# Two layers of MoE, attention and a gated recurrence: the recurrence as a pipeline over its blocks, its final state's product made once, loads and fills in another order, experts in a fixed order

## The chip, the cores and the metric

The kernel runs on one NeuronCore of a Trainium2 chip. Its engines are TensorE (PE, matrix products into PSUM), VectorE (DVE), ScalarE (ACT), GpSimd (POOL) and SyncE (SP, which here only issues DMAs); POOL issues DMAs too. The metric is the device time of one execution in microseconds, lower is better. All data are float32, and the profile shows each matmul of this kernel, other than the 128-column transposes, as two records.

## The reference, cut to what matters

x holds 2 x 2048 tokens of 256 values. Six sublayers are added to it in turn; the first and third, and the fourth and sixth, are the same function with the same weights.

```python
x = x + 0.5 * L0_ffn(layernorm(x))     # MoE: 6 experts, the best 2 per token, and a shared expert
x = x +       L0_attn(layernorm(x))    # attention, 16 heads, 2048 keys
x = x + 0.5 * L0_ffn(layernorm(x))
x = x + 0.5 * L1_ffn(layernorm(x))     # gated recurrence
x = x +       L1_attn(layernorm(x))    # causal attention with rotary and relative positions
x = x + 0.5 * L1_ffn(layernorm(x))
```

The recurrence runs over the first axis of x, which has only two entries, so it has two steps; each of the 2048 columns is on its own:

```python
def step(c, xt):
    ft = sigmoid(xt @ wf.T + c @ uf.T + bf)
    it = sigmoid(xt @ wi.T + c @ ui.T + bi)
    gt = tanh(xt @ wc.T + c @ uc.T + bc)
    return ft * c + it * gt
h = tanh(x @ wo.T + c_final @ uo.T + bo)   # c_final is the same for both steps
```

The MoE picks two experts per token, weights their outputs `(silu(x @ w1.T) * (x @ w3.T)) @ w2.T`, and adds a shared expert of the same form for every token.

## The kernel before

x stays in SBUF for the whole program, as 32 chunks of 128 tokens by 256 values; four chunks are a block (512 tokens), and there are eight blocks, four per batch entry. The stages follow one another in the order of the reference.

**Order of the work.** The program is traced in Python and a planner puts each engine's instructions in order: it simulates the program with estimated costs and at each point takes, of what is ready, what was written first. Inside `manual_schedule` the engines named there keep the written order. In the MoE that is PE alone, so DVE, ACT, POOL and SP are planned; the two attentions fix PE, ACT and DVE; the recurrence fixes none. SP and POOL are planned everywhere, and each engine executes its list in order. SBUF is taken in pools that are stacked: a pool that is opened where another was closed waits for the readers of the old one.

**MoE** (`first_moe`, `moe`; run twice). Tokens are treated in two halves of 16 chunks. `stats` and `norm` make the layer norm of a block and its transpose; `route` picks the experts; `sort` gives each (token, choice) a place in a list ordered by expert and scatters the normalised rows there with 32 indirect DMAs from POOL (L276) into `places`, a DRAM buffer. That buffer is set to zero once, by two DMAs from POOL at the start of the program (L1099), since some places stay empty. `shared` (up: L102, L290, L291) and `shared_down` (L299, L304) are the shared expert of a block. `experts` runs over 37 tiles of 128 places: load (L322, SP), transpose (L325, L327), up (L332, L337, L339), transpose of h (L344, L346), down (L351, L357), store to `results` (L358). `combine` gathers each token's two results with 32 indirect DMAs per half (L376, POOL) and adds them to x (L383, DVE). The written order is: halves' norms and routing with shared blocks 0 to 4 between, experts and combine of half 0, experts of half 1, shared blocks 5 to 7, combine of half 1.

**Recurrence** (`recurrence`; run twice). First six products give the gates' bias from the initial state (L694, L698). Then block after block (`cb`, the tokens of both steps): `layernorm_T` for both steps (L78 to L94), six gate banks a step (L102 from L719's loop, ACT at L719), the state on DVE (L722 to L731), and for each of 8 output chunks a sum in one bank of wo by x (L739), uo by the final state (L744) and a one-row product for the bias (L748); then tanh (L750) and the addition to x (L753). PSUM is used as three double banks and two single ones.

**Before attention 1.** Its weights are loaded, and two DRAM buffers `skew` are filled by 32 DMAs from POOL (L1144) ahead of the first recurrence. The recurrence's 13 weights are loaded in a pool of their own at the start of each of the two runs (L69).

Of the kernel before, what the change touches and what calls it, by code (L numbers as in the profile page):

```python
# [10 lines left out]
F32 = mybir.dt.float32  # L11
# [6 lines left out]
P = 128  # L18
# [24 lines left out]
def macaron_kernel(ctx: ExitStack, tc: tile.TileContext, t: dict, out: bass.AP):  # L43
# [5 lines left out]
    ones_row = const.tile([1, P], F32, name="ones_row")  # L49
    nc.vector.memset(ones_row, 1.0)  # L50
# [5 lines left out]
    nc.sync.dma_start(out=krow, in_=t["krow"])  # L56
# [6 lines left out]
    for b in range(NTB):  # L63
        nc.sync.dma_start(out=x[:, ts(b, CPB), :], in_=x_in[:, ts(b, CPB), :])

# [5 lines left out]

    def layernorm_T(c0, dst, lnp, psp, copy):


        mv = lnp.tile([P, CPB, 2], F32, name="mv")
        for c in range(CPB):
            st = lnp.tile([P, nc.vector.BN_STATS_DIM], F32, name="bnst")
            nc.vector.bn_stats(out=st, in_=x[:, c0 + c, :])  # L78
            nc.vector.bn_aggr(out=mv[:, c, :], in_=st)
        ve = lnp.tile([P, CPB], F32, name="ve")  # L80
        nc.gpsimd.tensor_scalar_add(ve, mv[:, :, 1], EPS)
        rstd = lnp.tile([P, CPB], F32, name="rstd")
        nc.gpsimd.tensor_tensor(rstd, ve, mhalf, ALU.pow)
        pair = psp.tile([P, 2, TB], F32, name="big")
        pts = [pair[:, kc, :] for kc in range(2)]
        for c in range(CPB):
            xn = lnp.tile([P, D], F32, name="xn")
            nc.vector.tensor_scalar(
                xn, x[:, c0 + c, :], mv[:, c, 0:1], rstd[:, c : c + 1], ALU.subtract, ALU.mult
            )  # L90
            for kc in range(2):
                nc.tensor.transpose(pts[kc][:, ts(c, P)], xn[:, ts(kc, P)], ident)
        for kc in range(2):
            copy(dst[:, kc, :], pts[kc])  # L94
# [16 lines left out]

    HB = NTB // 2
# [8 lines left out]
    def moe(w, ws, gate_w, gate_b, rev, tri, iota):  # L121
        with ExitStack() as s:
# [15 lines left out]
            mvs, rstds, oneh = {}, {}, {}  # L138
# [144 lines left out]
            def shared(b):  # L283
                pgu = [bank() for _ in range(4)]
                for i in range(4):
                    mm2(pgu[i], ws[:, :, i // 2 * D : i // 2 * D + D], ts(i % 2, P), xnT[b])
                hh = wk.tile([P, 2, TB], F32, name="hh", bufs=2)
                for ic in range(2):
                    sg = wk.tile([P, TB], F32, name="sgs", bufs=2)
                    nc.scalar.activation(sg, pgu[ic], AF.Silu)  # L290
                    nc.vector.tensor_tensor(hh[:, ic, :], sg, pgu[2 + ic], ALU.mult)  # L291
                return hh

            def shared_down(b, hh):
                for half in range(CPB // 2):
                    po = bank()
                    for c in range(2):
                        for ic in range(2):
                            nc.tensor.matmul(  # L299
                                po[:, ts(c, D)], lhsT=hh[:, ic, ts(half * 2 + c, P)],  # L300
                                rhs=ws[:, ic, 2 * D :], start=ic == 0, stop=ic == 1,
                            )
                    xs = x[:, ds(b * CPB + half * 2, 2), :].rearrange("p c d -> p (c d)")
                    nc.vector.scalar_tensor_tensor(xs, po, 0.5, xs, ALU.mult, ALU.add)  # L304

            def experts(h, exi):
# [54 lines left out]
                for i in range(NST + 2):  # L361
                    if i + 1 < NST:
                        tile_in(i + 1)
# [7 lines left out]
            def combine(h):  # L371
                for c in range(HC):
                    for i in range(2):
                        yg = wk.tile([P, D], F32, name="yg", bufs=6)
                        k = i * HC + c
                        nc.gpsimd.indirect_dma_start(  # L376
                            out=yg, out_offset=None, in_=results[h],
                            in_offset=bass.IndirectOffsetOnAxis(
                                ap=place[h][:, k : k + 1], axis=0
                            ),  # L380
                        )
                        xs = x[:, h * HC + c, :]
                        nc.vector.scalar_tensor_tensor(  # L383
                            xs, yg, weight[h][i][:, c, :], xs, ALU.mult, ALU.add
                        )

            with tc.manual_schedule(engines={mybir.EngineType.PE}):
                for b in range(HB):
                    stats(b)
                    norm(b)  # L390
                route(0)
                for b in range(HB, NTB):
                    stats(b)
                hh = [shared(0)]
                e0 = sort(0)
                for b in range(1, HB):
                    norm(HB + b - 1)
                    hh.append(shared(b))
                    shared_down(b - 1, hh[b - 1])
                norm(NTB - 1)  # L400
                route(1)
                hh.append(shared(HB))
                shared_down(HB - 1, hh[HB - 1])
                e1 = sort(1)
                shared_down(HB, hh[HB])
                experts(0, e0)
                combine(0)
                experts(1, e1)
                late = None
                for b in range(HB + 1, NTB):  # L410
                    hh = shared(b)
                    if late is not None:
                        shared_down(*late)
                    late = (b, hh)
                shared_down(*late)
                combine(1)
# [138 lines left out]
    ENGINES = {mybir.EngineType.PE, mybir.EngineType.Activation, mybir.EngineType.DVE}  # L555

# [123 lines left out]
    def recurrence(w):  # L680
        with ExitStack() as s:
# [3 lines left out]
            big = s.enter_context(tc.tile_pool(name="rec_big", bufs=3, space=PSUM))  # L685
            psp = s.enter_context(tc.tile_pool(name="rec_ps", bufs=2, space=PSUM))

            bias0 = {}
            for n in "fic":
                bias0[n] = keep.tile([P, 2], F32, name=f"bias0{n}")  # L690
                for m in range(2):
                    pb = psp.tile([P, TB], F32, name="ps1")
                    for kc in range(2):
                        nc.tensor.matmul(  # L694
                            pb[:, 0:1], lhsT=w[f"u{n}"][:, kc, ts(m, P)],
                            rhs=w["in_c"][:, kc : kc + 1], start=kc == 0, stop=kc == 1,
                        )
                    nc.vector.tensor_tensor(  # L698
                        bias0[n][:, m : m + 1], pb[:, 0:1], w[f"b{n}"][:, m : m + 1], ALU.add
                    )  # L700
            for cb in range(SB):
                xnT = []
                for step in range(2):
                    xt = wk.tile([P, 2, TB], F32, name=f"xnT{step}")
                    layernorm_T((step * SB + cb) * CPB, xt, lnp, big, nc.vector.tensor_copy)
                    xnT.append(xt)
                c1 = wk.tile([P, 2, TB], F32, name="c1")
                c2 = wk.tile([P, 2, TB], F32, name="c2")
                for step in range(2):
                    gate = {}  # L710
                    for n, fn in (("f", AF.Sigmoid), ("i", AF.Sigmoid), ("c", AF.Tanh)):
                        pg = big.tile([P, 2, TB], F32, name="big")
                        gate[n] = wk.tile([P, 2, TB], F32, name=f"g{n}")
                        for m in range(2):
                            mm2(pg[:, m, :], w[f"w{n}"], ts(m, P), xnT[step], stop=step == 0)
                            if step == 1:
                                mm2(pg[:, m, :], w[f"u{n}"], ts(m, P), c1, start=False)
                            bias = bias0[n] if step == 0 else w[f"b{n}"]
                            nc.scalar.activation(  # L719
                                gate[n][:, m, :], pg[:, m, :], fn, bias=bias[:, m : m + 1]  # L720
                            )
                    nc.vector.tensor_tensor(gate["i"], gate["i"], gate["c"], ALU.mult)  # L722
                    if step == 0:
                        for m in range(2):
                            nc.vector.scalar_tensor_tensor(
                                c1[:, m, :], gate["f"][:, m, :], w["in_c"][:, m : m + 1],
                                gate["i"][:, m, :], ALU.mult, ALU.add,
                            )
                    else:
                        nc.vector.tensor_tensor(c2, gate["f"], c1, ALU.mult)  # L730
# [507 lines left out]
```

## Time and profile before

| what | us |
|---|---|
| three runs | 4820.29, 4836.28, 4840.08 |
| median | 4836.28 |
| the profiled execution | 4831.55 |
| its span, first to last instruction | 4829.4 |

The stages in the profiled execution, cut where PE starts or ends them: start 0 to 42.5, first MoE to 413, way into attention 0 to 456.8, attention 0 to 2420, second MoE to about 2790, first recurrence from 2821.2 to 3066.6, attention 1 to 4563.3, second recurrence to 4829.4.

The profile's page gives each engine's busy time, the span in 40 slices with a digit of busy tenths, the granted TensorE clock, DMA queues, the chain of work that ended last, and groups of instructions with their mean duration and what they waited for. "L744 PE ... x4" is four instructions of line 744; a bracket at the end gives the idle time before them and the instruction that ended it. PEld is the load of weights into PE, which overlaps matmuls.

### The profile page before, as it was taken

The numbers are of one execution on the slowest core, as the hardware profiler recorded it, in microseconds if no ns is written. First come the engines' busy times: TensorE is split into PE (matmuls) and PEld (weight loads), VectorE is DVE, ScalarE is ACT, GpSimd is POOL, SyncE is SP. The second block draws the span as 40 slices with busy tenths as digits, with TensorE's granted clock in tenths as the row PEclk, the third lists the DMA queues.
The fourth block names the chain that finished last, engine by engine and source line by source line (L and its number), as shares of the span: only waits on it lengthen the run. The fifth ranks groups of instructions, "written<-read, shape, count | busy, mean of one in ns | idle before, by whom it ended". The sixth has DMA issues, their size and how long they took to land.

```text
span 4829.4 us, 74856 instructions
## 1 busy us (share of the span) xinstructions
PE 4579.8 (95%) x28768; PEld 2414.1 (50%) x28768; DVE 2649.7 (55%) x6138; ACT 2166.7 (45%) x4319; POOL 888.6 (18%) x925
## 2 busy tenths in 40 slices
PE   6996999999999999999989979899999999999999
PEld 3553544444444444444355535555555555555454
DVE  5234676767656667676452342356665555666421
ACT  2321465666655556566622211243544534445511
POOL 4315000002000000000043130343313344322000
PEclk9997999999999999999999989899999999999999
DMA  6331000000000000000033220244222244322100
GB/s 223 124 95 37 1 1 1 1 1 1 1 1 1 1 1 1 1 1 1 1 125 117 85 95 0 61 102 105 60 51 58 57 100 103 66 53 53 32 18 18
DMA packets 344904, 223.98 MB, mean 46 GB/s; under 512 B 146339, under 2 KB 324517, under 8 KB 344549
## 3 DMA queue, kind: packets, MB, share of 16 engines
q1 hardware_dynamic: 328324, 171.21, 14.0%
q0 software_dynamic: 16224, 47.99, 3.0%
q8 instruction: 229, 3.75, 0.3%
q14 instruction: 127, 1.03, 0.1%
HBM read 114.03 MB, written 105.12 MB: 45 GB/s over the span
## 4 chain that ended last, share of the span: by engine, by line
PE 88%; DVE 4%; POOL 3%; DMA 2%; issue 2%; ACT 0%; SPq 0%; POOLq 0%; DVEq 0%; ACTq 0%
PE s L615 15%; PE s L603 10%; PE acc L628 10%; PE s L852 7%; PE s L102 6%; PE s L937 6%; PE big L102 5%; PE acc L967 5%; PE s L332 5%; PE s L351 2%; PE ps L739 1%; PE ps L744 1%; DMA yg<-results,at 1%; PE s L547 1%; PE s L947 1%
## 5 line engine op out<-in xcount | busy, mean ns | idle before, releaser
L607 DVE TENSOR_REDUCE mx<-s 128x1 f32<-128x512 f32 x2048 | 1252.3, 683 | 597.7 <-PE s L603 597.5
L620 ACT ACTIVATE pT<-s 128x512 f32<-128x512 f32 x2048 | 1082.1, 601 | 628.5 <-PE s L603 582.9
L603 PE MATMUL s<-kT,q 32*128 32x512 f32 x4096 | 1249.9, 633 | 1.5 <-ACT q L596 1.4
L615 PE MATMUL s<-q,kT 32*128 32x512 f32 x4096 | 1231.7, 612 | 4.1 <-DVE q L512 4.1
L958 ACT ACTIVATE pT<-s 128x512 f32<-128x512 f32 (+3 forms) x1280 | 598.0, 544 | 500.0 <-PE s L937 290.6
L603 PEld LDWEIGHTS s<-kT,q 32*128 32x128 f32 x4096 | 539.2, 183 | 316.7 <-ACT pT L620 165.3
L852 PE MATMUL s<-kT,q 32*128 32x512 f32 (+6 forms) x3520 | 680.3, 473 | 9.7 <-POOL kT L790 7.4
L615 PEld LDWEIGHTS s<-q,kT 32*128 32x128 f32 x4096 | 500.5, 183 | 295.1 <-DVE mx L607 120.3
L860 DVE TENSOR_REDUCE mx<-s 128x1 f32<-128x512 f32 (+1 forms) x768 | 466.2, 677 | 253.7 <-PE s L852 234.3
L937 PE MATMUL s<-q,kT 32*128 32x512 f32 (+3 forms) x2048 | 522.3, 535 | 1.7 <-DVE s L991 1.7
L628 PE MATMUL acc<-pT,v 128*32 128x512 f32 x4096 | 492.3, 598 | 0.0
L852 PEld LDWEIGHTS s<-kT,q 32*128 32x128 f32 x3520 | 372.6, 188 | 110.4 <-ACT pT L958 31.7
L332 PE MATMUL s<-we,xT 128*128 x592 | 287.6, 609 | 0.9 <-ACT xT L327 0.9
L937 PEld LDWEIGHTS s<-q,kT 32*128 32x128 f32 x2048 | 231.6, 186 | 95.4 <-DVE mx L860 33.2
L967 PE MATMUL acc<-pT,v 128*32 128x512 f32 (+3 forms) x2560 | 268.5, 537 | 0.0
L628 PEld LDWEIGHTS acc<-pT,v 128*32 128x32 f32 x4096 | 107.2, 109 | 295.3 <-issue 294.1
L346 DVE COPY hT<-s 128x256 f32<-128x256 f32 x148 | 62.6, 424 | 292.7 <-PE s L344 292.7
L890 POOL TENSOR_TENSOR band<-band,mneg 128x640 f32<-128x640 f32 x128 | 160.9, 1260 | 313.9 <-DVE mneg L886 313.7
L876 DVE CUSTOM_DVE_ANT_0 band<-s,band 128x160 f32<-128x160 f32 (+1 forms) x512 | 155.5, 316 | 99.6 <-PE s L937 51.6
L147 POOL TENSOR_SCALAR ve<-mv 128x4 f32<-128x4 f32 x16 | 3.6, 226 | 1114.3 <-DVE mv L145 1110.3
L376 POOL DMA_INDIRECT yg<-results,at x128 | 121.5, 950 | 377.8 <-DMA results<-y 339.8
L351 PE MATMUL s<-we,hT 128*128 x592 | 157.1, 390 | 12.8 <-DVE hT L346 12.7
(209 smaller groups left out, 5052.5 us busy)
## 6 DMA issues: line engine op xcount, KB each, us to landing
band<-skew SPq DMA_DIRECT2D x32, 1280.0 KB, 6.6
pd<-band SPq DMA_DIRECT2D x32, 1280.0 KB, 8.1
xs<-places SPq DMA_DIRECT2D x148, 128.0 KB, 2.0
results<-y SPq DMA_DIRECT2D x148, 128.0 KB, 2.0
places<-zero POOLq DMA_DIRECT2D x2, 4736.0 KB, 36.2
we<-in_we SPq DMA_DIRECT2D x12, 768.0 KB, 10.2
skew<-s SPq DMA_DIRECT2D x32, 256.0 KB, 3.6
s<-pd SPq DMA_DIRECT2D x32, 256.0 KB, 3.5
```

Of the source, the lines that this page charges most:

```text
L102: nc.tensor.matmul(ps, lhsT=w[:, kc, cols], rhs=rhs[:, kc, :], start=start and kc == 0, stop=stop and kc == 1,)
L332: nc.tensor.matmul(pu, lhsT=xT[i][:, ts(kc, P)], rhs=w[:, kc, ds(val[i], 2 * D)], start=kc == 0, stop=kc == 1,)
L603: nc.tensor.matmul(ps, lhsT=q[t][rows(j), ts(qb, P)], rhs=kT[b, g][rows(j), ts(kc, TB)], start=True, stop=True,)
L607: nc.vector.tensor_reduce(mx[t][:, qb * J + j, kc : kc + 1], ps, AX.X, ALU.max)
L615: nc.tensor.matmul(st, lhsT=kT[b, g][rows(j), ts(kb, P)], rhs=q[t][rows(j), :], start=True, stop=True,)
L620: nc.scalar.activation(z.pTs[t, kb, j], st, AF.Exp)
L628: nc.tensor.matmul(z.acc[t][rows(j), :], lhsT=v[b, g // 2][:, kb, ds(h * VW, 32)], rhs=z.pTs.pop((t, kb, j)), start=kb == 0, stop=kb == NK ...
L852: nc.tensor.matmul(ps[:, ds(cols, n)], lhsT=lhsT, rhs=kT[b, c, g][rows(j), ds(k0, n)], start=True, stop=True,)
L860: nc.vector.tensor_reduce(m[:, c : c + 1], ps[:, 0:n], AX.X, ALU.max)
L937: nc.tensor.matmul(ps[:, q0:], lhsT=k, rhs=q[t][rows(j), q0:], start=True, stop=True, skip_group_check=True,)
L958: nc.scalar.activation(z.pTs[t, kb, j][:, q0:], st.pop((t, kb, j))[:, q0:], AF.Exp)
L967: nc.tensor.matmul(z.acc[t][rows(j), q0:], lhsT=v[b, kb // CPB, g // 2][:, kb % CPB, ds(h * VW, 32)], rhs=z.pTs.pop((t, kb, j))[:, q0:], s ...
```

## The change

- **Recurrence.** PE, ACT and DVE now run in written order. The layer norm (`normal`), its transposes (`turn`), the gates of one step and half of the state (`gate`), and the outputs are separate functions, written interleaved over blocks: gates of step 0 for the next block, layer norm of the one after, gates of step 1 for this block, outputs of the last block. The product of the final state with uo is made once a block in `final`, where DVE adds the bias (now stored for all 128 partitions), and DVE adds that sum to each step's product with wo; the one-row product is gone. All eight PSUM banks form one pool. In the second recurrence each pair of chunks is stored right after its last addition; before, the stores were written per block.
- **MoE.** PE, ACT and DVE in written order. The shared expert is cut into up, multiply and down; blocks 0 to 4 are put among the norms and routing. The combine of half 0 is written inside the experts of half 1, one chunk every second tile (`first_half`, from the fourth on); that of half 1 is spread among shared blocks 5 to 7.
- **Loads and fills.** The zero fill of `places` moves from POOL, ahead of everything, to SP, written behind the MoE's loads. Attention 0's weights are written behind the first MoE. The fill of `skew` moves from before the first recurrence, on POOL, to before the second MoE, on SP; the recurrence's first load of weights too is written before the second MoE. Attention 1's weights are allotted at the other end of SBUF.

```diff
-            with tc.manual_schedule(engines={mybir.EngineType.PE}):
+            with tc.manual_schedule(engines=ENGINES):
                 for b in range(HB):
                     stats(b)
                     norm(b)
+                    if b == 1:
+                        up(0)
                 route(0)
+                up(1)
+                mul(0)
+                e0 = sort(0)
+                mul(1)
+                down(0)
                 for b in range(HB, NTB):
+                    if b < NTB - 2:
+                        up(b - 2)
                     stats(b)
+                    norm(b)
+                    if b < NTB - 2:
+                        mul(b - 2)
+                        down(b - 3)
...
+                down(3)
+                up(4)
                 e1 = sort(1)
+                mul(4)
+                down(4)
+                experts(0, e0, lambda i: None)
+                experts(1, e1, first_half)
+                up(5)
+                mul(5)
+                up(6)
+                for c in range(6):
+                    combine(1, c)
+                down(5)
+                mul(6)
+                up(7)
+                for c in range(6, 11):
+                    combine(1, c)
+                down(6)
+                mul(7)
+                down(7)
+                for c in range(11, HC):
+                    combine(1, c)
...
+            def gate(cb, step, m):
+                g = {}
+                for n, fn in GATES:
+                    pg = bank()
+                    mm2(pg, w[f"w{n}"], ts(m, P), xnT[cb, step], stop=step == 0)
+                    if step == 1:
+                        mm2(pg, w[f"u{n}"], ts(m, P), c1[cb], start=False)
...
+            def final(cb):
+                cu = wk.tile([P, CPB, D], F32, name="cu")
+                for half in range(CPB // 2):
+                    po = bank()
+                    for c in range(2):
+                        for kc in range(2):
+                            nc.tensor.matmul(
+                                po[:, ts(c, D)], lhsT=c2[cb][:, kc, ts(half * 2 + c, P)],
+                                rhs=w["uo"][:, kc, :], start=kc == 0, stop=kc == 1,
+                            )
+                    nc.vector.tensor_tensor(
+                        cu[:, ds(half * 2, 2), :], po.rearrange("p (c d) -> p c d", c=2),
+                        w["bo"].to_broadcast([P, 2, D]), ALU.add,
+                    )
...
+            with tc.manual_schedule(engines=ENGINES):
+                normal(0)
+                first_bias()
+                for step in range(2):
+                    turn(0, step)
+                normal(1)
+                for m in range(2):
+                    gate(0, 0, m)
+                for step in range(2):
+                    turn(1, step)
+                for cb in range(SB):
+                    if cb + 1 < SB:
+                        for m in range(2):
+                            gate(cb + 1, 0, m)
+                    if cb + 2 < SB:
+                        normal(cb + 2)
+                    gate(cb, 1, 0)
+                    if cb + 2 < SB:
+                        for step in range(2):
+                            turn(cb + 2, step)
+                    gate(cb, 1, 1)
+                    if cb:
+                        outputs(cb - 1)
+                outputs(SB - 1)
...
     with tc.tile_pool(name="wa0", bufs=1) as wp:
-        weights = [load(wp, n) for n in ("a0_q", "a0_k", "a0_v", "a0_o", "a0_b")]
-        first_moe()
-        attention0(*weights)
-    first_moe()
+        first_moe(True)
+        attention0(*(load(wp, n) for n in ("a0_q", "a0_k", "a0_v", "a0_o", "a0_b")))
...
+    with tc.tile_pool(name="fill", bufs=1) as fp:
+        fill = fp.tile([P, UW], F32, name="fill")
+        nc.gpsimd.memset(fill[:, 0 : P + BAND], 0.0)
+        nc.gpsimd.memset(fill[:, P + BAND :], MASKED)
+        for n in range(2):
+            u = dram1.tile([CPB * J, P * UW], F32, name=f"skew{n}")
+            for m in range(CPB * J):
+                nc.sync.dma_start(out=u[m].rearrange("(r w) -> r w", w=UW), in_=fill)
+            skew.append(u)
     with ExitStack() as s:
+        early = s.enter_context(ExitStack())
+        rec = recurrence_weights(early.enter_context(tc.tile_pool(name="wr", bufs=1)))
+        first_moe(False)
+        wp = s.enter_context(tc.tile_pool(name="w1", bufs=1, side="right"))
...
-        run_recurrence()
+        recurrence(rec, False)
+        early.close()
         attention1(a, relk, relv, kbias, dramp, skew)
-    run_recurrence()
+    with tc.tile_pool(name="wr", bufs=1) as wr:
+        recurrence(recurrence_weights(wr), True)
```

## The prediction

> **What bounds the kernel.** The page comes first: busy shares and the 40 slices.
>
> ```profile
> span 4829.4 us, 74856 instructions
> PE 4579.8 (95%) x28768; PEld 2414.1 (50%) x28768; DVE 2649.7 (55%) x6138; ACT 2166.7 (45%) x4319; POOL 888.6 (18%) x925
> ...
> PE   6996999999999999999989979899999999999999
> ...
> PEclk9997999999999999999999989899999999999999
> ```
>
> TensorE (PE) is the bound; what can be won is either work taken from PE or its dips. Second, the busy time of each engine by stage, with cuts where a stage's first or last PE instruction stands (columns: stretch, its us, then busy us of each engine with the count, granted clock, DMA share, GB/s):
>
> ```profile
> 0.00:42.50 42.50, 0.00 (x0) 0.00 (x0) 14.37 (x71) 1.28 (x1) 12.72 (x23) 1.00 0.97 362
> 42.50:108.30 65.80, 64.40 (x256) 39.45 (x257) 36.87 (x124) 20.14 (x33) 33.19 (x35) 1.00 0.41 153
> 108.30:222.40 114.10, 113.86 (x453) 70.31 (x452) 34.88 (x109) 37.18 (x109) 30.68 (x32) 1.00 0.39 124
> 222.40:361.30 138.90, 123.81 (x454) 74.10 (x455) 43.08 (x107) 39.34 (x113) 30.58 (x32) 0.94 0.32 98
> ...
> 2756.80:2821.20 64.40, 31.16 (x98) 18.10 (x96) 28.02 (x70) 3.96 (x7) 49.59 (x68) 0.77 0.55 174
> 2821.20:3066.60 245.40, 234.57 (x696) 124.50 (x696) 70.73 (x155) 43.59 (x65) 15.93 (x23) 0.94 0.03 9
> ```
>
> The two attentions (1963 and 1469 us) are PE at 98 to 99%, and the diff leaves them alone. The rest is about 1400 us: an idle start of 42.5 us at 362 GB/s; the second half's experts 25 us longer than the first's, with the same 37 tiles; a hole before the recurrence; two recurrences (245 and 266 us) busy, yet at a clock of 0.94 and 0.90. Third, the timeline where a recurrence block ends:
>
> ```profile
> 4803.34 1.13 PE L744 MATMUL ps<-uo,c 128*128 128x256 f32 x4 [2.87 <-DVE c L731]
> 4804.40 0.69 PE L748 MATMUL ps<-bo,ones_row 1*128 1x256 f32 x2
> 4805.03 2.07 PE L739 MATMUL ps<-wo,xnT 128*128 128x256 f32 x4
> 4806.89 1.81 PE L744 MATMUL ps<-uo,c 128*128 128x256 f32 x4
> ```
>
> PE waits 2.87 us for the state, and later quartets take 1.8 to 2.1 us, not 1.13: the wait costs clock too. Fourth, waits and hole:
>
> ```profile
> PE s L344 <- DVE h L339: 8.3, 5, 2.7
> PE s L351 <- DVE hT L346: 6.5, 4, 2.3
> ```
> ```profile
> 2803.72 15.39 POOL L1144 DMA_DIRECT2D skew<-fill  x29 [1.72 <-issue]
> 2821.18 2.28 PE L92 MATMUL big<-ident,xn 128*128 128x128 f32 x8 [33.24 <-DVE xn L88]
> ```
>
> **Recurrence, product made once.** A block has 8 output chunks (2 steps x 4). Before, a chunk takes 4 records of wo, 4 of uo and 2 of the bias; in the last block's timeline chunks start 2.55 us apart (0.96 + 0.96 + 0.63), so 8 x 2.55 = 20.4 us. After: 32 records of wo and 16 of uo at 0.24 = 11.5 us. Saved 8.9 a block, 36 us a recurrence. The added 2 + 4 additions (0.69 each) and the tanh that now waits for one lie on DVE and ACT: with two layer norms DVE comes to about 30 us a block, ACT 12, against PE's 44.5 (72 gate records at 0.43 = 30.9, 16 transposes at 0.13 = 2.1, outputs 11.5). Without that cover a block's four outputs take 4 x 2.2 us on DVE (0.69 + 0.60 + 0.69 and hand-overs), as they will at the very end: +1.5 us.
>
> **Recurrence, pipeline.** PE work before is 4 x 53.4 + 3 for the first bias = 216.5 of 245.4 us: 29 us are waits and lost clock. After, 4 x 44.5 = 178. What is late next: DVE runs a layer norm pair (normal, 10.4 us: twice 1.9 statistics, 1.7 wait for POOL, 1.5 scaling) in order, while PE covers it with one gate of 24 records (10.3 us), so turn waits some 1.2 us, three times. With a cold first stretch I charge 7 us. The clock is where the Trainium skill speaks against the gain: "TensorE: Matmul & The Clock Gate", Part 1, puts the loss of clock after an idle window of about 3.4 us, so a wait of 2.87 us should cost only itself. The row shows 0.52 and 0.63 granted in the 4 us after it. By the rule only PE's idle time of the stage (245.4 - 234.6 = 11 us) goes with the waits; the other 18 would be slow matmuls that stay, 18 x 178/216.5 = 15 us a recurrence, a forecast 30 us later. By the row the 18 are what the waits leave behind, and go with them. I take the row.
> First recurrence, from the last experts matmul (2756.8): it ended 309 us later (3065.9). After: combine needs 4 + 32 gathers x 1.25 and landing; its fixed places among shared hold the last gathers by some 3 us, so 51; normal(0) 10.4 (nothing covers it), turn and copy 1.6; 178 + 7. Sum 248, gain 61. The skew fills no longer hold POOL for 15 us ahead of rstd. Against it: attention1's first statistics, which the planner had slipped into the recurrence's DVE stream, now stand behind all of it: 1.9 + 1.6 + 4.84 for POOL's xn: +7. The a1 loads (11 DMAs, SP) wait for MoE space; a scaling of a_q placed ahead of normal(0) would hold DVE: 0 to 6 us, I take 2, as SP is free then.
> Second, from 4563.3: weights issue in 6 us and land by 4573 under normal(0); gates from 4578.5; 178 + 7; tail 7 (before 5.7): 4770.5 against 4829.4, gain 59.
>
> **Start.** x (4.2 MB) shared 362 GB/s with the zero fill (9.7 MB), which stood first on POOL. Alone it takes 12 us, gate and shared weights land by 17, experts' by 31, the fill behind them on SP by 43 and 57. The Trainium skill ("DMA: Bandwidth & Descriptors", Issuing engines are not separate DMA queues) says that another issuing engine saves only issue time: true of the sum, 15.4 MB by 42.5 us, yet order is what x gains from; by the rule alone I would write 0. Next bound: up(0) runs from 18, when ws is there, to 25 (16 records at 0.43); two norms, 28; route 2.9, then up(1) 6.9 beside route's DVE chain (5.5 in the timeline at 52 to 58 us), 38; sort's product and DVE chain 7.5. So sort(0) is ready about 45.5, its scatter takes 32 x 1.265 = 40.5 and may not start before the first fill lands; PE's own 65.6 us from 18 end beside it. Experts start near 89, not 108.3: -19. Bounds: -8, if a scatter waits for both fills, and -27.
>
> **Experts.** In the second half combine(0) stands on DVE between h and hT, waiting for gathers 1.25 us apart; now one chunk every two steps (6 us of PE against 2.5 of gathers). Stage to 114: -25, and -22 in the second MoE (136.3). If a gather comes late, DVE blocks as now and PE loses up to those 25 us again; at the first, step 3 falls 10 us after the half's end, and its two gathers land 9.5 after it (4.5 for results, 2 x 1.25, 2.5), so the margin is thin there and grows by 3.5 us a chunk. Closing combine: +3 in the first MoE, as in the second (counted above); attention0's own start (POOL xn, 4.84 us a block) follows it as before.
>
> **Second MoE's loads.** 32 fills move from POOL to SP, where 12 MoE loads (and 13 of the recurrence) stand: 32 x 0.43 = 14 us issue. The first L69 load in 2420.2 waited for the pool's last reader (L547), so I take it that the fill does too. Then ws lands about 2441, and up(0), now written early, waits: in PE's fixed order norm(2), route and sort follow it. Scatter +5. Bounds: -9 (MoE loads go first), +12 (recurrence weights too go first). I take +3.
>
> **At nothing.** The stores are 16 of half the size, all but the last under later matmuls; bo grows from 1 to 128 KB (0.4 us at 362 GB/s, under normal); the fill's memsets go to POOL while it has no other work; krow behind x is wanted in attention0; shared's parts in a new order add no work, and PE's queue is full there (64.4 of 65.8 us).
>
> **Sum.** -61 +7 +2 -59 -19 -25 +3 +3 -22 = -171. The profiled execution took 4831.55 us (span 4829.4 and 2.1 around it); less 171 is 4660. The median of the runs, 4836.28, is 4.7 higher, inside their spread of 20: I forecast 4662.
>
> **Rivals.**
> *Waits remain in the recurrence* (8 PSUM banks in turn, two gate buffers, DVE in order): only the product is won, 72 us plus the hole: +38, 4700. For: 29 us of waits were there with three double banks. Against: DVE has 14 us free a block.
> *SP does not follow the written order*: the planner already issued a_q at 43.63, behind the expert loads that it was written ahead of (its pool may have waited for the zero tile, whose fill ended about then; the trace doesn't tell which). Then fills or recurrence weights stand before what PE needs: start 0, second MoE +18: 4662 + 19 + 15 = 4696.
> *Slower*: fixing DVE and ACT in the experts puts hT(i-1) behind h(i) in each tile. If every one of 148 tiles paid one such wait (1.6 us, the mean of the 9 above), 148 x 1.6 = 237: 4899. It decides from 171/148 = 1.16 us a tile. Against: in the first half's experts hT follows 2.0 to 2.3 us of idle DVE, and down of a tile comes two steps after up.
> *More*: MoE loads first, no turn waits, attention1 not delayed: 4625.
>
> **Chances.** Forecast 0.64 (own range 4630 to 4690), waits remain 0.14, SP order 0.13, more 0.07, slower 0.02. From these 4612 to 4720 holds 8 in 10. A measurement of this kernel tells from 0.5% (24 us) on: faster 0.97, same 0.01, slower 0.02.
>
> **What would show it.** L744's successor 64 records instead of 128 a recurrence and no K=1 records; each recurrence about 185 us PE at clock 1.00; experts stages both near 114; first PE work at 8 to 18 us; experts from 89; no hole of 33 us before the first recurrence. Wrong if experts tiles exceed 3.0 us, turn waits over 3 us, or ws lands after 2450.

## The result, and the profile after

The changed kernel takes 4759.62 us (median of four runs, 4759.19 to 4762.41), the kernel before 4836.14 us beside it: a ratio of 0.9849, with a 95% interval of 0.9827 to 0.9871. It is faster by 76 us where 174 were forecast, and lies outside the range of 4612 to 4720. Its profiled span is 4757.5 us.

The page first, the span, PE's busy time, and the slices of PE and of its granted clock:

```profile
span 4757.5 us, 74391 instructions
PE 4465.8 (94%) x28512; PEld 2373.6 (50%) x28512; DVE 2690.3 (57%) x6193; ACT 2179.9 (46%) x4339; POOL 872.2 (18%) x893
...
PE   4996999999999999999975998899999999999999
...
PEclk7997999999999999999987998999999999999999
```

PE is busy for 114 us less, but the span fell by 72 only, so the idle time of PE has grown by 42 us. The first slice (119 us) fell from 6 to 4, and the clock of its first slice from 9 to 7; a second dip has grown where the second MoE begins. The stages say it in numbers (columns: stretch, its us, busy us and count of PE, PEld, DVE, ACT, POOL, granted clock, DMA share, GB/s):

```profile
0.00:46.50 46.50, 32.28 (x113) 17.72 (x114) 26.07 (x101) 13.38 (x19) 6.01 (x16) 1.00 1.01 348
46.50:148.90 102.40, 46.08 (x162) 28.88 (x161) 38.08 (x127) 10.90 (x17) 42.52 (x47) 0.70 0.30 103
...
261.40:374.20 112.80, 112.46 (x446) 69.29 (x446) 42.08 (x106) 38.29 (x111) 32.04 (x32) 1.00 0.39 120
2433.10:2596.10 163.00, 79.65 (x273) 47.30 (x273) 64.61 (x227) 22.99 (x35) 47.90 (x57) 0.72 0.32 111
...
2708.70:2821.50 112.80, 112.47 (x446) 69.26 (x446) 42.10 (x106) 38.18 (x111) 31.80 (x32) 1.00 0.39 120
2871.00:3063.60 192.60, 177.15 (x544) 99.81 (x544) 88.35 (x205) 47.16 (x72) 18.05 (x24) 0.95 0.03 10
4560.20:4757.50 197.30, 180.36 (x569) 104.71 (x568) 86.08 (x188) 48.29 (x73) 10.12 (x16) 0.96 0.10 33
```

The start up to 46.5 us, the second halves of the experts (112.8 us each) and the two recurrences are what was forecast or better. The two openings of the MoE are not: between 46.5 and 148.9 PE works 46 of 102 us, and from 2433.1 on 80 of 163. A ledger over the whole span, cut at the same PE instructions in both traces (the first transposes of the experts' tiles, at 111.8 and 148.9 us in the first MoE; the last down product of a half; attention 0's last product; the last product of a recurrence and of attention 1):

| step | forecast | before, us | after, us | measured |
|---|---|---|---|---|
| first MoE's opening | -19 | 111.8 | 148.9 | +37.1 |
| its experts, first half | 0 | 112.6 | 112.5 | -0.1 |
| its experts, second half | -25 | 137.1 | 112.8 | -24.3 |
| its closing, and attention 0 | +3 | 2058.5 | 2058.9 | +0.4 |
| second MoE's opening | +3 | 87.7 | 163.0 | +75.3 |
| its experts, first half | 0 | 112.6 | 112.5 | -0.1 |
| its experts, second half | -22 | 136.7 | 112.8 | -23.9 |
| its closing and the first recurrence | -61 +2 | 308.9 | 242.1 | -66.8 |
| attention 1 with its start | +7 | 1497.4 | 1496.6 | -0.8 |
| second recurrence | -59 | 266.1 | 197.3 | -68.8 |

The forecasts sum to -171, the measurements to -72. The openings miss by 128 us; all the rest is 29 us better than forecast.

What PE waits for in the second opening (columns: us in all, times, longest):

```profile
PE s L137 <- DVE xn L130: 54.1, 5, 38.7
PE s L76 <- DMA ws<-in_ws: 18.7, 1, 18.7
PE s L278 <- DVE hh L271: 9.1, 1, 9.1
PE s L157 <- ACT lgT L154: 1.4, 2, 0.7
```

Here `xn` are the normalised rows, `ws` the shared expert's weights, `hh` the product inside the shared expert. In the first opening, up to 200 us, the same list has 58.0 for the normalised rows (longest 38.9), 9.1 for `hh` and 2.0 for `ws`. The timeline of the first shows where the longest wait comes from:

```profile
46.49 1.24 POOL L251 DMA_INDIRECT places<-xn,at  x1 [23.14 <-DVE ex L242]
48.03 0.96 POOL L251 DMA_INDIRECT places<-xn,at  x1 [0.30 <-issue]
...
85.97 0.96 POOL L251 DMA_INDIRECT places<-xn,at  x1 [0.30 <-issue]
86.97 0.25 POOL L122 TENSOR_SCALAR ve<-mv 128x4 f32<-128x4 f32 x1
87.30 1.05 POOL L124 TENSOR_TENSOR rstd<-ve,mhalf 128x4 f32<-128x4 f32 x1
88.38 1.38 DVE L130 TENSOR_SCALAR xn<-x,mv,rstd 128x256 f32<-128x256 f32 x4 [35.73 <-POOL rstd L124]
...
88.94 2.21 PE L137 MATMUL s<-ident,xn 128*128 128x128 f32 x8 [38.88 <-DVE xn L130]
```

POOL issues 32 scatters from 46.5 to 87, and only then the rstd of block 4 (what its rows are scaled by in the layer norm), 1.3 us of work. DVE, in its fixed order, stands still for 35.7 us at that block's layer norm, and PE for 38.9 us. In the kernel before the last two rstd stood ahead of the first scatter:

```profile
42.54 2.24 POOL L149 TENSOR_TENSOR rstd<-ve,mhalf 128x4 f32<-128x4 f32 x2
66.47 1.13 POOL L276 DMA_INDIRECT places<-xn,at  x1 [21.68 <-DVE at L264]
```

There the statistics of blocks 4 to 7 are also written ahead of `sort(0)`, right behind `route(0)`; the change writes them behind it. The second opening has the wait for `ws` besides. SP's queue there (columns: start, us of issue):

```profile
2433.25 0.33 SPq L67 DMA_DIRECT2D gate_w<-in_gate_w  x1
2433.68 16.28 SPq L1200 DMA_DIRECT2D skew<-fill  x32
...
2459.13 0.33 SPq L67 DMA_DIRECT2D in_c<-in_in_c  x1
2459.79 0.33 SPq L67 DMA_DIRECT2D ws<-in_ws  x1
```

The fills and all 13 weights of the recurrence stand between `gate_w` and `ws`.

The recurrence, by contrast, has lost its holes. The end of a block, where the kernel before waited 2.87 us and then ran slow quartets:

```profile
3042.84 3.62 PE L768 MATMUL s<-uo,state 128*128 128x256 f32 x16
3046.29 7.07 PE L782 MATMUL s<-wo,xnT 128*128 128x256 f32 x32
```

No bracket stands behind these lines: PE waits for nothing, and a record takes 0.216 us (3.45/16, by the starts). From 3000 to 3060 PE is busy 60.00 of 60 us at a clock of 1.00.

### The profile page after: what moved, and what is told of

It is laid out like the page before. It is cut to its first block, busy times and chain, and to the rows that moved or that the text cites. A ratio compares the mean times of both kernels' runs of the same rounds, so it can differ in the third digit from the quotient of the medians.

```text
span 4757.5 us, 74391 instructions
## 1 busy us (share of the span) xinstructions
PE 4465.8 (94%) x28512; PEld 2373.6 (50%) x28512; DVE 2690.3 (57%) x6193; ACT 2179.9 (46%) x4339; POOL 872.2 (18%) x893
## 5 line engine op out<-in xcount | busy, mean ns | idle before, releaser
L925 PE MATMUL s<-kT,q 32*128 32x512 f32 (+5 forms) x3520 | 678.4, 471 | 9.5 <-POOL kT L863 7.4
L318 DVE TENSOR_TENSOR h<-sg,s 128x256 f32<-128x256 f32 x148 | 62.3, 421 | 303.7 <-ACT sg L316 303.7
```

The costliest lines, as they stand in the source:

```text
L925: nc.tensor.matmul(ps[:, ds(cols, n)], lhsT=lhsT, rhs=kT[b, c, g][rows(j), ds(k0, n)], start=True, stop=True,)
```

## The experiments

**Theory A**: the statistics of blocks 4 to 7 were moved behind the first sort in the text, and with DVE's order fixed their rstd gets behind 40 us of scatters on POOL. **Theory B**: the fixed order of PE, DVE and ACT with the new order of the parts costs the time by itself. **Theory C**: in the second MoE it is the loads' order. All runs compute everything that the kernel before computes.

### 1. Statistics early

```diff
                 for b in range(HB):
                     stats(b)
+                    stats(HB + b)
                     norm(b)
...
-                    stats(b)
                     norm(b)
```

> Only the statistics of blocks 4 to 7 are moved: each is written next to that of block b - 4, ahead of the sort of the first half, instead of behind it. Theory A (POOL's queue: the rstd of blocks 4 to 7 stands behind the 32 scatters, 40 us, and DVE, PE and the rest of the MoE's opening wait for it): experts start near 90 instead of 149 in the first MoE, and 50 us sooner in the second, so about 4650 us (4635 to 4675). Theory B (the fixed order of DVE and ACT, or the new order of shared's parts on PE, costs the time itself): no more than 15 us won, 4745 or more. Theory C (in the first MoE POOL, in the second the loads' order on SP): 60 us won in the first alone, about 4700.

Measured: 4668.16 us (4667.68 to 4669.11), 91 us under the kernel after; ratio to before 0.966 (0.9643 to 0.9677). Experts start at 104.6 us in the first MoE and 115.1 us after attention 0 in the second, 44 and 48 us sooner. That is in the range of theory A; B and C fall. The start at 90 was missed, though; the waits of PE up to 105 us say by what:

```profile
PE s L137 <- DVE xn L130: 18.8, 4, 13.4
PE s L278 <- DVE hh L271: 9.2, 1, 9.2
```

The 38.9 us are gone. 13.4 us is now the very first wait (the statistics of block 4, written ahead of the first norm, wait for that block of x; in the kernel after PE began at 8.9), and 9.2 us is a second, smaller case of the same kind: the multiplication of shared block 4 stands behind the second sort on DVE.

### 2. The second MoE's loads first

```diff
             for e in range(NE):
                 nc.sync.dma_start(out=w[:, :, ts(e, EW)], in_=t["we"][:, :, ts(e, EW)])
+            if behind:
+                behind()
...
+        def behind():
+            fill = fp.tile([P, UW], F32, name="fill")
...
+            rec.update(recurrence_weights(wr))
+            for n in range(2):
+                u = dram1.tile([CPB * J, P * UW], F32, name=f"skew{n}")
+                for m in range(CPB * J):
+                    nc.sync.dma_start(out=u[m].rearrange("(r w) -> r w", w=UW), in_=fill)
+                skew.append(u)
+        first_moe(False, behind)
```

> Only SP's order is changed: in the second MoE its own 12 loads come first, then the recurrence's 13 weights, then the 32 fills. Theory A: PE's wait of 18.7 us for ws falls to about 4, the rest of the second opening stays (rstd behind the scatters), so some 15 us won, 4745 (4738 to 4752). Theory C: the loads are what makes the second MoE's opening 76 us longer, so 60 to 75 won, about 4690.

Measured: 4743.28 us (4741.27 to 4745.31), 16 us under the kernel after. The second opening is 142.6 us instead of 163.0. As A expected; the loads are a part of the second opening's loss, and the smaller one. (The opening is 20 us shorter, the whole time 16.)

### 3. Both

The two edits together.

> Both moves together. Theory A: the two add, about 4634 us (4620 to 4655); experts start near 90 in the first MoE and about 87 us after attention0's last matmul in the second, as in the kernel before. Theory B: 4735 or more, the 15 us of the loads and little else. If sorting takes over as the bound (40 us of scatters from about 46 us on), the first MoE stops at 90 and gives no more.

Measured: 4650.03 us (4647.88 to 4651.21), 110 us under the kernel after; the single gains sum to 108, so the two are independent. The expected range is met at its upper end, again for the 9.2 us behind the second sort, which PE now waits in each MoE, and the late first norm.

### 4. Only POOL's order

```diff
                     stats(b)
+                    scatter(0, range(8 * (b - HB), 8 * (b - HB) + 8))
                     norm(b)
...
-            with tc.manual_schedule(engines=ENGINES):
+            with tc.manual_schedule(engines=ENGINES | {mybir.EngineType.Pool}):
```

> The orders of PE, DVE and ACT stay exactly as in the kernel after; only on POOL (whose order is fixed too, inside the MoE) the rstd of block 4 goes ahead of the first half's scatters, and those of blocks 5 to 7 after 8, 16 and 24 of them. Theory A: the wait of 36 us for the rstd of block 4 goes, each block then waits for at most 10 us of scatters beside PE's own 10 us a block; experts start near 102 and some 45 us sooner in the second MoE, about 4668 us (4650 to 4690). Theory B (order on DVE, ACT, PE is the cost): as the kernel after, 4750 to 4770.

Measured: 4708.79 us (4707.43 to 4711.76), 51 us under the kernel after, with not one instruction of PE, DVE or ACT in another place: B is excluded as the whole cause, the queue of POOL is shown. The size was missed (experts start at 123.3, not 102). The waits up to 124 us (line numbers are each run's own: L276 here is the product `hh` that was L271 before):

```profile
PE s L137 <- DVE xn L130: 30.9, 5, 9.3
PE s L283 <- DVE hh L276: 9.2, 1, 9.2
```

The batches of eight scatters became waits of up to 9.3 us each. The expectation had counted on PE's 10 us a block to lie beside them; in its order only one up product of 7.0 us stands ahead of the transposition that waits, and all else of the block behind it.

### 5. The multiplication ahead of the second sort

```diff
                 up(4)
-                e1 = sort(1)
                 mul(4)
+                e1 = sort(1)
                 down(4)
```

On top of run 3.

> Both moves of before, and one line: shared's multiplication of block 4 is written ahead of the second half's sort instead of behind it. In the trace with both moves PE waits 9.2 us in each MoE for that product, behind the sort's chain on DVE. Theory A (DVE's fixed order, one chain after the other): the wait goes, and the next bound is the first half's last scatter (ends near 90.3 us, landing about 4 us later), so 5 to 9 us won in each MoE: about 4635 us (4630 to 4642). Theory B (scatters or the places' first load already set the start of the experts): 4647 to 4651, no gain.

Measured: 4628.95 us (4628.34 to 4633.03), 21 us under run 3, a little more than expected. Experts start at 93.8 us in the first MoE and 85.6 us after attention 0 in the second. In the waits up to 94 us the next bound appears:

```profile
PE s L137 <- DVE xn L130: 18.7, 4, 13.3
PE s L304 <- DMA xs<-places: 1.4, 1, 1.4
```

PE now waits 1.4 us for the first sorted tile: work and scatters end together.

### 6. The product made once, alone in the kernel before

```diff
+                cu = wk.tile([P, CPB, D], F32, name="cu")
+                for half in range(CPB // 2):
+                    po = psp.tile([P, TB], F32, name="ps1")
...
+                    nc.vector.tensor_copy(
+                        cu[:, ds(half * 2, 2), :], po.rearrange("p (c d) -> p c d", c=2)
+                    )
                 for step in range(2):
...
+                        nc.vector.tensor_tensor(
+                            hs, po, cu[:, ds(half * 2, 2), :].rearrange("p c d -> p (c d)"), ALU.add
+                        )
+                        nc.scalar.activation(hs, hs, AF.Tanh)
```

The bias stays a one-row product here, but is made once a block too, so half of these records go as well.

> The kernel before with one part alone: in its recurrence the product of the final state (with the bias, still a K=1 record) is made once a block, copied to SBUF, and added on DVE to each step's product; the loop stays as it was, serial, with the planner's order. A block has 16 records of uo and 8 of the bias fewer: 16 x 0.24 + 8 x 0.31 = 6.3 us, 50 us in all. Theory P (the product is worth its records, the waits and the clock stay): 4786 us (4775 to 4798). Theory Q (PE waits behind it grow, since DVE now has 6 more instructions a block and stands in the chain): 4805 or more. Theory R (most of the recurrence's 136 us is the product): below 4765.

Measured: 4765.65 us (4763.39 to 4766.65), 70 us under the kernel before, between P and R and next to R's limit of 4765. The removed records were worth more than their fast duration, because in that place they were slow: over the first recurrence before, 128 records of uo have 37.5 us (0.293 each) and 64 of the bias 23.8 us (0.372 each). 128 and 64 fewer over the two recurrences make 61 us. The 256 records of wo, which all stay, got faster besides: 62.0 us over both recurrences instead of 81.7. The end of a block in this run shows why records are slow (L739 is uo by the final state here, L743 the bias):

```profile
4728.45 1.88 PE L102 MATMUL big<-c,uc 128*128 128x512 f32 x4
4733.63 2.07 PE L739 MATMUL ps<-uo,c 128*128 128x256 f32 x4 [3.30 <-DVE c L731]
4735.63 1.22 PE L743 MATMUL ps<-bo,ones_row 1*128 1x256 f32 x2
4736.78 2.08 PE L739 MATMUL ps<-uo,c 128*128 128x256 f32 x4
```

A wait of 3.30 us, and then quartets of 2.08 us at a granted clock of 0.50, which lasts to 4749.7 us.

### 7. The pipeline alone

```diff
-                cu = final(cb)
                 for step in range(2):
+                    cu = final(cb)
                     for half in range(CPB // 2):
```

In the kernel after.

> The kernel after with the product of the final state made twice a block again, once for each step, in the pipeline as it is. 16 records a block more at 0.216 us: 3.5 us a block, 28 in all, so 4788 us (4783 to 4795) where PE is the only bound of the recurrence. Theory R (most of the recurrence's 136 us is the product): 4830 or more. If DVE is near its limit in the pipeline, its two more additions a block add up to 11 us: 4799.

Measured: 4789.67 us (4786.92 to 4792.04), 30 us over the kernel after: 128 records at 0.216 us are 27.6. So in the pipeline the product is worth 30 us. Run 6's 70 are not the same thing: they hold half of the one-row records too. Nor is run 7 the pipeline alone: its bias stays on DVE, so it has no one-row records at all. By the ledger both parts together win 136; run 6 wins 70, run 7 by difference 106 (136 - 30), which is 40 too many. The busy time of the records, in us over both recurrences, says what is in both:

| records | before | run 6 | run 7 | after |
|---|---|---|---|---|
| one-row products (bias) | 49.1 | 26.4 | 0 | 0 |
| uo by the final state | 78.9 | 42.4 | 57.9 | 28.9 |
| wo by x | 81.7 | 62.0 | 57.9 | 56.4 |

Counted in both are 23 us of one-row records (49.1 - 26.4), 18 of wo, which either run makes faster (19.7 + 23.8 - 25.3), and 8 of uo: 49 us of busy time, of which 40 show in the time. No run removes the one-row products alone, so what they are worth by themselves stays open.

### 8 and 9. Three further waits, and their better half

```diff
-        nc.vector.tensor_scalar_mul(a["q"], a["q"], 0.25)
...
         recurrence(rec, False)
+        nc.vector.tensor_scalar_mul(a["q"], a["q"], 0.25)
+        nc.vector.tensor_tensor(kbias, kbias, krow, ALU.add)
...
-                "wf", "uf", "wi", "ui", "wc", "uc", "wo", "uo", "bf", "bi", "bc", "bo", "in_c",
+                "in_c", "uf", "ui", "uc", "bf", "bi", "bc", "wf", "wi", "wc", "bo", "uo", "wo",
```

On top of run 5; in the first of the two, `stats(HB + b)` stands behind `norm(b)` as well.

> The kernel of the mul moved first, and three further waits: the statistics of blocks 4 to 7 stand behind the norm of block b - 4 (so that the first norm doesn't wait for a later block of x), DVE's scalings of the attention's weights are written behind the first recurrence instead of ahead of it, and the recurrence's weights are loaded in the order of their use, in_c first. Worked out: 0 to 4 at the start, some 8 ahead of the first recurrence (DVE waits 3.7 and 3.0 for a_q and relv there), 3 to 8 ahead of the second (PE waits 9.9 for in_c, DVE's layer norm takes about as long): 4635 less 14 is about 4621 us (4612 to 4632). If attention1 starts later by the scalings: 4630.

Measured: 4622.23 us (4621.41 to 4623.57), 7 us under run 5. The scalings' move is worth its price: PE's wait for the first recurrence's first layer norm is 5.85 us instead of 15.81 in the kernel after, and from the last expert product to that transposition it takes 50.0 us, 60.8 in run 5. The loads in order of use help the second recurrence: PE waits 3.17 us there for its first weights, 11.32 in run 5, and the recurrence is 7 us shorter. But the statistics behind the norm start the experts later, at 95.9 us, and 92.0 us after attention 0.

> As the run of the three further waits, but with the statistics of blocks 4 to 7 next to those of block b - 4 again (filling DVE's wait for the rstd), since behind the norm they cost 2 us in the first MoE's opening and 6 in the second's by the traces; the scalings behind the recurrence and the loads in order of use stay. If the traces' differences add: 4622.2 - 2.1 - 6.3 = 4614 us (4610 to 4619). If instead the later start of the experts only took up a wait for the scatters: 4620 to 4624.

Measured: 4612.25 us (4611.59 to 4614.03), 17 us under run 5; experts at 93.8, and 85.7 us after attention 0. The traces' differences add. This is the fastest kernel of the study: ratio to before 0.9543 (0.9527 to 0.9559), 147 us under the kernel after.

### 10. Only PE's order fixed

```diff
-            with tc.manual_schedule(engines=ENGINES):
+            with tc.manual_schedule(engines={mybir.EngineType.PE}):
```

In the MoE of the kernel after.

> The kernel after with only PE's order fixed inside the MoE, as it was before; DVE and ACT are left to the planner there, everything else (written order of parts, gathers between the experts' tiles) as in the kernel after. The planner then puts the statistics of blocks 4 to 7, and on POOL their rstd, ahead of the scatters. Theory A (it is the fixing of DVE's order behind which the statistics stand): the openings win what the early statistics won, 91 us, and the wait behind the second sort goes too if the planner brings that product forward: 4650 to 4672 us. For the experts' second half: 112.6 us as after, if the place of the gathers in the text is what won 26 us there; 130 or more, if the fixed order of DVE did, and then about 4700.

Measured: 4701.65 us (4701.47 to 4704.98), the second of the two cases. Experts start at 98.0 us and 105.9 us after attention 0, 51 and 57 us sooner: left to itself, DVE does the statistics before the sort, and so does POOL. But the experts' second halves take 133.9 and 135.5 us. What DVE does there:

```profile
245.72 0.49 DVE L361 SCALAR_TENSOR_TENSOR x<-yg,col,x 128x256 f32<-128x256 f32 x1 [0.91 <-DMA yg<-results,at]
247.48 0.48 DVE L361 SCALAR_TENSOR_TENSOR x<-yg,col,x 128x256 f32<-128x256 f32 x1 [1.27 <-DMA yg<-results,at]
249.63 0.48 DVE L361 SCALAR_TENSOR_TENSOR x<-yg,col,x 128x256 f32<-128x256 f32 x1 [1.66 <-DMA yg<-results,at]
250.03 0.41 DVE L318 TENSOR_TENSOR h<-sg,s 128x256 f32<-128x256 f32 x1
```

The planner has put three additions of gathered rows, each waiting for its DMA, ahead of one h that PE needs. The new place of the gathers in the text alone is worth 3.2 and 1.2 of the 24 us there; the rest takes the fixed order too. The row points at DVE, though DVE and ACT were freed together here, and a fixed order with the gathers in their old place was not run. The same fixed order, with the statistics written behind the sort, lost 108 us in the openings.

### 11. The fill behind the loads, alone in the kernel before

```diff
-            nc.gpsimd.dma_start(
-                out=places[h].rearrange("(n p) d -> p n d", p=P),
-                in_=zero.to_broadcast([P, NST, D]),
-            )
...
+            if clear:
+                zero = wp.tile([P, 1, D], F32, name="zero")
+                nc.gpsimd.memset(zero, 0.0)
+                for h in range(2):
+                    nc.sync.dma_start(
+                        out=places[h].rearrange("(n p) d -> p n d", p=P),
+                        in_=zero.to_broadcast([P, NST, D]),
+                    )
```

> The kernel before with one part alone: the fill of the places goes from POOL's queue, ahead of everything, to SP's, behind the first MoE's loads. Theory S (x gains from the order of the transfers): x has landed by about 12 us instead of 42, PE begins at 9 instead of 42.5; then the loads of attention0 (2.2 MB), gate, ws, experts (4.7 MB) and the first half's fill follow, at 362 GB/s by about 49 us, the first scatter waits for it, 32 of them take 40.5 us: experts start near 94 instead of 108 to 112, so 15 to 19 us won, 4818 us (4812 to 4824). Theory T (the sum of the bytes sets the start[...]): 4830 or more.

Measured: 4813.17 us (4799.98 to 4821.50), ratio 0.9955 (0.9939 to 0.997). PE begins at 10.5 us and the experts at 94.5, 17.3 sooner than before. Theory S. The first MoE's start was forecast rightly as far as the transfers go.

## Why the prediction was wrong

**The step that failed** is the sentence under "At nothing": "shared's parts in a new order add no work, and PE's queue is full there (64.4 of 65.8 us)", and its use under "Start": "PE's own 65.6 us from 18 end beside it". The working named `sort(0)`'s 40.5 us of scatters and PE's 65.6 us as two things side by side. The scatters began at 46.5 us, as it had them (45.5). In the diff, though, the statistics of blocks 4 to 7 have moved behind `sort(0)`, and their rstd is an instruction of POOL. Fixed DVE could not bring them forward any more, and so PE's 65.6 us had a piece of POOL's queue in the middle. It takes both, the moved text and the fixed order: run 1 puts the statistics back, run 10 frees DVE and ACT, and either one starts the experts 44 to 57 us sooner. Of the openings' miss of 128 us, run 1 takes back 92 (by the trace), with nothing but the statistics moved; run 4 takes back 50 with POOL's order alone. Another 18 is the same thing on a smaller scale, the multiplication behind the second sort (9.1 us in each MoE, run 5), and 20 are the loads' order (run 2, by the trace of the opening): 130 in all. The prediction asked what would stand behind what for SP's queue and for the experts' h and hT; for DVE and POOL in the openings it did not ask.

**Second MoE's loads: right sign and mechanism, wrong size.** I wrote "Bounds: -9 (MoE loads go first), +12 (recurrence weights too go first). I take +3". The weights did go first, and PE waited 18.7 us for `ws`, more than the bound; the order cost 16 us (run 2). The fills, put at 14 us of SP, took 16.3, and the 13 weights 7.7 us more, ahead of `ws`. The named sign, `ws` after 2450, came true.

**Start: right, and covered up.** The forecast for the start, "Experts start near 89, not 108.3: -19", was 111.8 to 93.8 in run 5, -18.0, and -17.3 with the fill alone (run 11). x gained from its place in the queue of transfers: PE began at 10.5 us in run 11, 42.5 before. That is in accord with the choice made against the rule in the Trainium skill, "DMA: Bandwidth & Descriptors", Issuing engines are not separate DMA queues: the sum of bytes is the rule's, their order is the kernel's.

**Experts: right** (-25 and -22 against -24.3 and -23.9). A tile took 3.04 us (112.5/37) in all halves (over the 3.0 that was named as a sign of being wrong, but the forecast's own 114/37 is 3.08, so that sign says nothing); the rival *slower* had hT behind h cost 1.6 us a tile, and it cost nothing.

**Recurrences: right mechanism, 16 us too little** (-120 forecast, -135.6 measured). Two terms were too high: a record of the outputs took 0.216 us, not 0.24 (384 records, 9 us), and PE waited at most 0.28 us in a turn, not 1.2 (six turns, 5.5 us). The rival *waits remain* is out. The Trainium skill, "TensorE: Matmul & The Clock Gate", Part 1, with its idle window of about 3.4 us, would have left 30 us of slow matmuls in place. The runs decide for the row: after a wait of 3.30 us in run 6 the clock was 0.50, and without waits (and without one-row products) it was 1.00 for the products with uo and wo (after, and run 7). That page also calls the window free-running; that where a pause lies in it decides what the pause costs, no run here tests.

**Ahead of the recurrence: two errors that cancelled.** DVE's scalings of the attention's weights, taken at 2 us (0 to 6), held the first layer norm by 10.7 (run 8 against run 5, 60.77 - 50.04 from the last expert product to the first transposition). The rest, combine and layer norm, took 50, not 61.4. Attention 1's start lost nothing where +7 was charged: the planner still found a place for its first statistics.

**In sum**: 4662 with the openings' miss of +128 and the rest's -29 is 4761; measured 4760. Of the rivals, *SP does not follow the written order* (4696) is out at the start, where SP issued x, the loads and the fill as they are written. In the second MoE the fills and the weights did stand ahead of `ws`, as it said, but there they are written ahead of it too. It says nothing of POOL, where the larger cost lay.

## What to carry to other kernels

Fixing an engine's order makes every instruction of it wait for the slowest queue that feeds any earlier one: for each instruction that moves, list what it needs from the engines whose order is not fixed, and what stands ahead of that there. Issue long runs of indirect DMAs on POOL after the small arithmetic that others wait for. And a removed product is worth its duration in its own surroundings: two edits that take away some of the same records, or both cure slow ones, must not be added up.

## What the runs showed of the hardware that was not expected

- A scatter of 128 rows holds POOL for 0.96 us and the gap of 0.30 behind it, so 32 of them shut POOL for 40.5 us to all arithmetic behind them.
- A wait of 3.30 us was followed by a granted clock of 0.50 for 16 us of full work in run 6 (4733.6 to 4749.7), one of 2.87 us in the kernel before for only 3.4 us (4805.1 to 4808.5). The traces have a regularity here. In the outputs of the recurrences there are eight stretches at 0.50 (six before, two in run 6). In the five where one-row products stood among the others, the clock stayed at 0.50 as long as they did, and 3.4 to 5.9 us longer (13.7 or 17.1 us in all); in the three with next to none it was back at 1.00 after 3.4 us. At 1.00 the same mix did not lower it. The lines have the granted clock third from the end: first the kernel before (one-row products up to 4750.4, again from 4753.9, none from 4805.1 to 4808.4), then run 6 (up to 4746.3, then none):

```profile
4740.20:4753.80 13.60, 13.60 (x29) 7.98 (x27) 0.72 (x2) 0.60 (x1) 0.00 (x0) 0.50 0.00 0
4753.90:4757.30 3.40, 3.40 (x14) 2.20 (x14) 0.69 (x1) 0.60 (x1) 0.00 (x0) 1.00 0.10 34
4805.10:4808.40 3.30, 3.30 (x8) 2.45 (x8) 0.00 (x0) 0.00 (x0) 0.00 (x0) 0.50 0.00 0
```
```profile
4733.60:4746.20 12.60, 12.57 (x24) 6.69 (x24) 0.69 (x1) 0.00 (x0) 0.00 (x0) 0.50 0.00 0
4746.30:4749.70 3.40, 3.40 (x9) 2.77 (x9) 0.69 (x1) 0.00 (x0) 0.00 (x0) 0.50 0.00 0
4749.80:4753.10 3.30, 3.30 (x17) 2.92 (x16) 1.98 (x3) 0.93 (x2) 0.00 (x0) 1.00 0.00 0
```

That the one-row products keep the clock low is what this suggests; no run was made to test it.
